# Cross-attention on one core: weights loaded ahead of the context, G made first, Wv and x in pieces of 256 bytes, U in tiles of 32 columns

## The chip, the cores and the metric

One core of a Trainium2 chip, one launch. The time is the device time of an execution in microseconds (us). A kernel's time is the median of its runs. One further execution is profiled; its span, from the first to the last instruction on the core, is a little shorter than its time.

## The reference, cut to what matters

```python
# x: 16 x 256 x 256, ctx_768: 16 x 77 x 192, 8 heads of D = 256, all float32
Q = (x @ Wq).reshape(B, -1, H, D).transpose(0, 2, 1, 3)          # Wq: 256 x 2048
K = (ctx_768 @ Wk).reshape(B, -1, H, D).transpose(0, 2, 1, 3)    # Wk: 192 x 2048
V = (ctx_768 @ Wv).reshape(B, -1, H, D).transpose(0, 2, 1, 3)    # Wv: 192 x 2048
score = jnp.einsum('bhqd,bhkd->bhqk', Q, K) / math.sqrt(D)
score = jnp.where(mask, score, -jnp.inf)
attn = jax.nn.softmax(score, axis=-1)
ctx = jnp.einsum('bhqk,bhkd->bqhd', attn, V).reshape(B, -1, H * D)
out = ctx @ Wo + x                                                # Wo: 2048 x 256
mu = jnp.mean(out, axis=-1, keepdims=True)
var = jnp.var(out, axis=-1, keepdims=True)
return (out - mu) * jax.lax.rsqrt(var + EPS) * gamma + beta
```

## The kernel before, in words

The kernel multiplies the weights with each other first. For each head, G = Wk Wq^T (192 x 256, scaled) and U = Wv Wo (192 x 256). Then the scores are x (G^T c^T), with c the context, and the output is the softmax's weights times (c U). So the work has a **prologue**, which makes G and U once, and a **main loop** over the 16 batches.

The order of every engine's work is the order in which the code issues it (`manual_schedule`, line 83): an engine runs its instructions in order, and each waits on semaphores for what it needs. There are no due times. Transfers are issued by SP, a few by ACT, also in order. Eight completion semaphores are used in turn by the transfers, so an issue waits until the transfer eight before it has landed. PSUM is one pool of eight banks (`ps_mm`, line 92), taken in turn.

The prologue, by lines:

- Loads: the context `c_sb` (449, the first two of 11 row groups by ACT; 450 the rest by SP), then per pair of heads Wq and Wk (458, 459; the first pair in two halves), then Wv in 24 transfers of 64 KB (463), Wo in four of 512 KB (471), the mask, and x of the first four batches (155, eight transfers of 128 KB, by `load_xT`). Wv and x are loaded in blocks of 32 x 32 elements, pieces of 128 bytes, so that VectorE (DVE) can transpose the blocks in place (584, 164).
- `keep_busy` (480 to 484, 487): 22 transposes of the identity into a bank that nobody reads.
- The context's transposes on PE, `pc` (492), with copies to `cA` by ACT, to the upper half of `cB` by DVE, and to its lower half by POOL (498 to 503).
- `turn_qk` (531): per head, four transposes of Wq (`p_wqT`) and four of Wk (`p_wkT`), all at line 524, each with one copy (ACT and DVE in turn, `evacuate`, 135). `pg` (538): two products for rows 0 to 127 of a head's G, issued after the next head's transposes. `ph` (548): the other 64 rows of G, two heads side by side in one bank, tiles of 64 columns.
- `prepare_a` (169) for the first four batches: `pa` (186 from `cA` and `gA`, 200 from `cB` and `gB`). DVE transposes Wv's blocks between the copies (584).
- `pu` and `pw` (538, 548): U by the same helpers, `of_weights` and `rest_of_weights`. Then `pr` (265, 273): the part of c U for the last 13 keys of each batch, which goes by way of DRAM (`scratch`, 287) to `vr` (292).

The helpers for the matrices' shapes: a product "128*32" uses 128 rows and 32 columns of PE's array; four of them beside each other fill the 128 columns. `pa`, `pv`, `ps` and `po` are made in such tiles (BK = 32).

The main loop (632 to 682): per batch the scores `ps` (306) of its two tiles of 128 queries, the softmax on DVE, POOL and ACT, `pv` (228, 239: c U of the batch), `pa` of a batch four ahead, `po` (371), and the normalisation. x of the next four batches is loaded (653) and transposed (671) inside it, and the residual `xg` (131) is loaded four times 1 MB after the prologue's other loads. The tiles `xg` lie on the buffers of the transposed Wq and Wk (510 to 515).

Of the kernel before, what the change touches and what calls it, by code (L numbers as in the profile page):

```python
# [1 line left out]

# [14 lines left out]
P = 128  # L17
# [28 lines left out]
def kernel(  # L46
# [102 lines left out]
    def load_blocks(dst, src):  # L149

        dst = dst.rearrange("p a (m q) -> p a m q", q=BK)
        src = src.rearrange("(m r) (a i q) -> a i r m q", r=BK, q=BK, i=P // BK)
        for a in range(dst.shape[1]):
            for i in range(P // BK):
                nc.sync.dma_start(dst[i * BK : (i + 1) * BK, a], src[a, i])

    def load_xT(g):
        xT_of[g] = in_two("xT", [P, 2, GT * P], g)
        load_blocks(xT_of[g], x.rearrange("b s d -> (b s) d")[g * GT * P : (g + 1) * GT * P, :])

    def transpose_x(g, j):

        cols = xT_of[g][:, :, j * P : (j + 2) * P]
        nc.vector.transpose(cols, cols)
# [4 lines left out]
    def prepare_a(g, pairs, B_first=False):  # L169
# [8 lines left out]
        def cols(dc, i):  # L178
            return slice(dc * P + i * BK, dc * P + (i + 1) * BK)
# [118 lines left out]
    def scores(t):  # L298
# [3 lines left out]
        for m in range(NM):  # L302
            q = j * P + m * BK
            for dc in range(2):
                for i in range(NM):
                    nc.tensor.matmul(  # L306
                        ps[m // 2][i * BK : (i + 1) * BK, m % 2 * 2 * S2 : (m % 2 + 1) * 2 * S2],
                        xT_of[g][:, dc, q : q + BK],
# [134 lines left out]
    with tc.tile_pool(name="wload", bufs=4) as ring, tc.tile_pool(name="wonce", bufs=1) as wp:  # L443
# [3 lines left out]
        wo_r = wo.rearrange("(t p) f -> p t f", p=P)  # L447
        first = 2
        nc.scalar.dma_start(c_sb[:, :first, :], c_rows[:, :first, :])
        nc.sync.dma_start(c_sb[:, first:, :], c_rows[:, first:, :])  # L450
        wq_of, wk_of, wo_of = {}, {}, {}
        wvT = wp.tile([P, H, 2, DL], F32, tag="wvT", name="wvT")
        for n in range(NF):
            wq_of[n] = ring.tile([P, 2, 2 * D], F32, tag="w128", name=f"wq_{n}")
            wk_of[n] = ring.tile([LP, 2, 2 * D], F32, tag="w96", name=f"wk_{n}")
            for lo, hi in ((0, D), (D, 2 * D)) if n == 0 else ((0, 2 * D),):
                cols = slice(2 * n * D + lo, 2 * n * D + hi)
                nc.sync.dma_start(wq_of[n][:, :, lo:hi], wq_r[:, :, cols])
                nc.sync.dma_start(wk_of[n][:, :, lo:hi], wk_r[:, :, cols])
        wv_blocks = wv.rearrange("(m r) (a i q) -> m i r a q", r=BK, q=BK, i=NM)  # L460
        for m in range(DL // BK):
            for i in range(NM):
                nc.sync.dma_start(
                    wvT.rearrange("p h a l -> p (h a) l")[
                        i * BK : (i + 1) * BK, :, m * BK : (m + 1) * BK
                    ],
                    wv_blocks[m, i],
                )
        for n in range(NF):
            wo_of[n] = ring.tile([P, 4, DI], F32, tag="w128", name=f"wo_{n}")  # L470
            nc.sync.dma_start(wo_of[n], wo_r[:, 4 * n : 4 * n + 4, :])
# [12 lines left out]
        keep_busy(20)  # L484
        for r in range(0, NCR, 2):
            if r == first:
                keep_busy(2)
            n = min(2, NCR - r)
            pc = ps_mm.tile([P, 4, P], F32, tag="mm", name=f"pc_{r}")
            for lc in range(2):  # L490
                for j in range(n):
                    nc.tensor.transpose(
                        pc[:, 2 * lc + j, :CR],
                        c_sb[:, r + j, lc * LB : lc * LB + P],
                        ident[:CR, :CR],
                    )
            rows = slice(r * CR, (r + n) * CR)
            evacuate(flat(cA)[:, rows].rearrange("p (j m) -> p j m", m=CR), pc[:, :n, :CR])
            evacuate(
                flat(cB)[LB:, rows].rearrange("p (j m) -> p j m", m=CR),  # L500
                pc[LB:, 2 : 2 + n, :CR],
            )
            nc.gpsimd.tensor_copy(flat(cB)[:LB, rows], flat(cB)[LB:, rows])
        nc.gpsimd.tensor_copy(cRA, cA[:, :, KM:])
        nc.gpsimd.tensor_copy(cRB, cB[:, :, KM:])

# [219 lines left out]
```

## Time and profile before

| | |
|---|---|
| median of 3 runs | 290.67 us (290.23 to 291.16) |
| profiled execution | 290.27 us |
| its span | 288.4 us |
| mean granted PE clock | 0.992 |
| bytes moved | 25.90 MB; 46905 of 64377 packets under 512 bytes |

In the lists, PE is TensorE's products, PEld its weight loads (which run beside products), DVE VectorE, ACT ScalarE, POOL GpSimd, SP the queue that issues transfers. A float32 product appears as two instructions, a transpose as one, so "x32" at line 538 is sixteen products. A line such as `L538 PE MATMUL pu<-wo,wvT 128*128 128x256` reads: line 538, on PE, writes tile pu from tiles wo and wvT, array 128 x 128, moving operand 128 partitions by 256 elements. "[0.80 <-DMA wk]" is idle time of that engine just before, and what ended it. "issue" means that nothing the profile shows was waited for. The chain of work that ended last is followed back from the last instruction, each time to what released it.

### The profile page before, as it was taken

The page shows a single profiled execution, that of the slowest core. Times are in us where ns is not written, and L with a number is a line of the kernel's source. Part 1 is how long each engine was busy: PE and PEld are TensorE (multiplying, and loading weights), DVE is VectorE, ACT ScalarE, POOL GpSimd, SP SyncE. Part 2 cuts the span into 40 slices and gives each one's busy share as a digit, 9 for nine tenths or more (in the row PEclk, how much of TensorE's full clock was granted, in tenths as well). Part 3 has the DMA queues.
Part 4 walks back from the last instruction along what each step waited for, and adds up shares of the span by engine and source line. Part 5 has one row for each costly group of instructions (what it writes and reads, how often), then busy time and mean ns, then how long its engine had stood idle before and what let it go on. Part 6 is the DMA issues. An engine that isn't in the chain of part 4 may idle for free.

```text
span 288.4 us, 11416 instructions
## 1 busy us (share of the span) xinstructions
PE 278.7 (97%) x5132; PEld 177.5 (62%) x5132; DVE 206.3 (72%) x412; ACT 118.2 (41%) x203; POOL 123.7 (43%) x156
## 2 busy tenths in 40 slices
PE   8899999999999999999999999999999999999990
PEld 8795567364656575757575757575757567576550
DVE  0531453435768798989797989897979898898884
ACT  2452232032353535353535353535353534735531
POOL 1800002986554334344334242534342527658562
PEclk9999999999999999999999999999999999999996
DMA  7986798895859401910101009200000000010112
GB/s 201 314 193 95 143 328 117 244 352 147 189 141 139 81 4 39 139 47 5 37 5 35 6 28 142 47 13 25 18 22 22 19 22 24 19 40 2 39 39 73
DMA packets 64377, 25.90 MB, mean 90 GB/s; under 512 B 46905, under 2 KB 62857, under 8 KB 64329
## 3 DMA queue, kind: packets, MB, share of 16 engines
q1 hardware_dynamic: 64088, 25.01, 36.8%
q8 instruction: 40, 0.66, 1.0%
q10 hardware_dynamic: 240, 0.17, 0.2%
q14 instruction: 9, 0.07, 0.1%
HBM read 19.27 MB, written 5.90 MB: 87 GB/s over the span
## 4 chain that ended last, share of the span: by engine, by line
PE 90%; DVE 3%; DMA 3%; SPq 1%; ACT 1%; issue 1%; POOL 0%; POOLq 0%
PE ps L306 23%; PE po L371 22%; PE pa L186 12%; PE pv L228 10%; PE pa L200 6%; PE pv L239 6%; DMA wk<-in_L_xattn_Wk_dram 3%; PE pu L538 2%; PE pr L265 2%; PE pg L538 2%; PE pr L273 1%; PE ph L548 1%; PE pw L548 1%; PE p_wqT L524 1%; PE p_wkT L524 1%; DVE bn L385 1%
## 5 line engine op out<-in xcount | busy, mean ns | idle before, releaser
L328 POOL TENSOR_TENSOR s<-s,top 128x616 f32<-128x616 f32 x32 | 39.0, 1218 | 85.0 <-DVE top L327 77.2
L306 PE MATMUL ps<-a,xT 128*32 128x154 f32 x2048 | 70.0, 294 | 0.0
L306 PEld LDWEIGHTS ps<-a,xT 128*32 128x32 f32 x2048 | 66.4, 110 | 4.0 <-ACT stage L138 0.8
L349 POOL TENSOR_TENSOR p<-e,rden 128x512 f32<-128x512 f32 x64 | 50.4, 808 | 28.6 <-ACT a L664 25.5
L371 PE MATMUL po<-vw,pT 128*32 128x256 f32 x1024 | 61.5, 380 | 0.0
L371 PEld LDWEIGHTS po<-vw,pT 128*32 128x32 f32 x1024 | 31.8, 110 | 28.2 <-issue 5.5
L341 DVE TENSOR_REDUCE den<-e 128x8 f32<-128x616 f32 x32 | 25.5, 795 | 24.2 <-ACT e L335 24.2
L335 ACT ACTIVATE e<-s 128x616 f32<-128x616 f32 x32 | 23.0, 719 | 32.1 <-POOL s L328 32.1
L186 PE MATMUL pa<-cA,gA 128*32 128x308 f32 x512 | 35.8, 423 | 0.0
L320 DVE TENSOR_TENSOR s<-ps,bias 128x308 f32<-128x308 f32 x64 | 27.6, 464 | 7.3 <-POOL bias L617 4.7
L662 ACT COPY vw<-pv 128x512 f32<-128x512 f32 x32 | 18.6, 581 | 32.2 <-PE pv L239 32.2
L228 PE MATMUL pv<-uA,cA 128*32 128x512 f32 x256 | 30.4, 592 | 0.0
L186 PEld LDWEIGHTS pa<-cA,gA 128*32 128x32 f32 x512 | 16.4, 110 | 21.0 <-issue 6.6
L428 DVE SCALAR_TENSOR_TENSOR xg<-xg,rstd,bet 128x256 f32<-128x256 f32 x26 | 28.0, 1078 | 0.9
L396 ACT ACTIVATE std<-mv,eps 128x2 f32<-128x2 f32 (+1 forms) x17 | 5.0, 296 | 57.2 <-DVE mv L388 57.2
L359 DVE STREAM_TRANSPOSE pT<-p 128x640 f32<-128x640 f32 x32 | 25.1, 812 | 2.4 <-POOL p L349 2.4
L327 DVE TENSOR_REDUCE top<-s 128x8 f32<-128x616 f32 x32 | 25.4, 795 | 1.1
L371 PE MATMUL po<-vr,pT 128*32 128x256 f32 x256 | 19.7, 379 | 0.0
L396 ACT ACT_TABLE_LOAD x15 | 19.2, 1283 | 0.3
L200 PE MATMUL pa<-cB,gB 64*32 64x308 f32 x512 | 19.3, 419 | 0.0
L335 ACT ACT_TABLE_LOAD x14 | 18.0, 1283 | 0.2
L599 POOL COPY uB<-uB 64x256 f32<-64x256 f32 x8 | 3.2, 397 | 34.7 <-ACT uB L598 34.3
(75 smaller groups left out, 288.2 us busy)
## 6 DMA issues: line engine op xcount, KB each, us to landing
xT<-in_x_dram SPq DMA_DIRECT2D x32, 128.0 KB
xg<-in_x_dram SPq DMA_DIRECT2D x4, 1024.0 KB
out_dram<-xg SPq DMA_DIRECT2D x15, 256.0 KB
wo<-in_L_xattn_Wo_dram SPq DMA_DIRECT2D x4, 512.0 KB
scratch<-stage SPq DMA_DIRECT2D x16, 104.0 KB
vr<-scratch SPq DMA_DIRECT2D x8, 208.0 KB
wq<-in_L_xattn_Wq_dram SPq DMA_DIRECT2D x3, 512.0 KB
wvT<-in_L_xattn_Wv_dram SPq DMA_DIRECT2D x24, 64.0 KB
```

The costliest lines, as they stand in the source:

```text
L186: nc.tensor.matmul(flat(o[i * BK : (i + 1) * BK]), gA[:, h, cols(dc, i)], flat(cA[:, batches, :]), start=not B_first, stop=B_first,)
L200: nc.tensor.matmul(flat(banks[j + k][i * BK : (i + 1) * BK]), gB[half(k), h // 2, cols(dc, i)], flat(cB[half(k), batches, :]), start=B_fir ...
L228: nc.tensor.matmul(pv[k][i * BK : (i + 1) * BK], cA[:, b, k * BK : (k + 1) * BK], flat(uA[:, heads[i], :]), start=True, stop=False,)
L306: nc.tensor.matmul(ps[m // 2][i * BK : (i + 1) * BK, m % 2 * 2 * S2 : (m % 2 + 1) * 2 * S2], xT_of[g][:, dc, q : q + BK], flat(a_of[g][:, ...
L320: nc.vector.tensor_tensor(s[:, a * H // 2 : (a + 1) * H // 2], ps[a][:, : H // 2 * S2].rearrange("p (h k) -> p h k", k=S2), bias[:, b, :]. ...
L327: nc.vector.tensor_reduce(top, s, AX.X, ALU.max)
L328: nc.gpsimd.tensor_tensor(s, s, top.unsqueeze(2).to_broadcast([P, H, S2]), ALU.subtract)
L335: nc.scalar.activation(e, s_of.pop(t), AF.Exp)
L341: nc.vector.tensor_reduce(den, e, AX.X, ALU.add)
L349: nc.gpsimd.tensor_tensor(part, e_mh[:, :, :, keys], rden_mh.unsqueeze(3).to_broadcast(list(part.shape)), ALU.mult,)
L371: nc.tensor.matmul(po[i * BK : (i + 1) * BK], pT[:, n, i], vw_of[b][:, n // 2, n % 2, :] if n < NF else vr[:, b, :], start=(n == 0), stop= ...
L428: nc.vector.scalar_tensor_tensor(y, y, rstd, bet, ALU.mult, ALU.add)
```

## The change

- **Order.** Wq is loaded by SP and Wk by ACT, ahead of the context, which is now one transfer by SP. PE starts with `turn_qk(0)` and makes G's rows 0 to 127 for all heads and the first half of `ph` before the context's transposes `pc`; the second half of `ph` follows them. `keep_busy` issues ten transposes at the start and none later.
- **Order of d, pieces.** Of a head's 256 values of d, partition block i of 32 holds 64i to 64i + 63, in two parts of 32, in place of 32i to 32i + 31 of each half. So a piece of Wv or x is 64 contiguous elements, 256 bytes. Wv has 24 transfers of the same 64 KB; x has 4 of 256 KB for four batches in place of 8 of 128 KB. `prepare_a` takes G's columns, and Wo's rows are loaded, in this order: Wo comes in 16 transfers of 128 KB (pieces of 1 KB), into one tile `wo_all`, which lies on the buffer of `wq_all` (one tag, one buffer).
- **U in tiles of 32.** `of_weights` has a width: 128 for G, 32 for U. `rest_of_weights` uses 32 for both. U then has 64 products of 128*32 for `pu` in place of 16 of 128*128, and 32 for `pw` in place of 16 of 128*64; `ph` too has 32 in place of 16.

The diff, cut (the helpers that only move are left out):

```diff
     def load_xT(g):
-        xT_of[g] = in_two("xT", [P, 2, GT * P], g)
-        load_blocks(xT_of[g], x.rearrange("b s d -> (b s) d")[g * GT * P : (g + 1) * GT * P, :])
+        xT_of[g] = in_two("xT", [P, GT * NM, 2, BK], g)
+        rows = x.rearrange("b s d -> (b s) d")[g * GT * P : (g + 1) * GT * P, :]
+        rows = rows.rearrange("(m r) (i n) -> i r m n", r=BK, i=NM)
+        for i in range(NM):
+            nc.sync.dma_start(
+                xT_of[g][i * BK : (i + 1) * BK].rearrange("p m n q -> p m (n q)"), rows[i]
+            )
...
         def cols(dc, i):
-            return slice(dc * P + i * BK, dc * P + (i + 1) * BK)
+            return slice((2 * i + dc) * BK, (2 * i + dc + 1) * BK)
...
-                        xT_of[g][:, dc, q : q + BK],
+                        xT_of[g][:, j * NM + m, dc],
...
-        nc.scalar.dma_start(c_sb[:, :first, :], c_rows[:, :first, :])
-        nc.sync.dma_start(c_sb[:, first:, :], c_rows[:, first:, :])
-        wq_of, wk_of, wo_of = {}, {}, {}
-        wvT = wp.tile([P, H, 2, DL], F32, tag="wvT", name="wvT")
+        wk_of = {}
+        wq_all = wp.tile([P, NF, 2, 2 * D], F32, tag="w128", name="wq_all")
+        wq_of = [wq_all[:, n] for n in range(NF)]
+        wvT = wp.tile([P, H, DL // BK, 2, BK], F32, tag="wvT", name="wvT")
         for n in range(NF):
-            wq_of[n] = ring.tile([P, 2, 2 * D], F32, tag="w128", name=f"wq_{n}")
             wk_of[n] = ring.tile([LP, 2, 2 * D], F32, tag="w96", name=f"wk_{n}")
             for lo, hi in ((0, D), (D, 2 * D)) if n == 0 else ((0, 2 * D),):
                 cols = slice(2 * n * D + lo, 2 * n * D + hi)
                 nc.sync.dma_start(wq_of[n][:, :, lo:hi], wq_r[:, :, cols])
-                nc.sync.dma_start(wk_of[n][:, :, lo:hi], wk_r[:, :, cols])
-        wv_blocks = wv.rearrange("(m r) (a i q) -> m i r a q", r=BK, q=BK, i=NM)
+                nc.scalar.dma_start(wk_of[n][:, :, lo:hi], wk_r[:, :, cols])
+        nc.sync.dma_start(c_sb, c_rows)
+        wv_blocks = wv.rearrange("(m r) (h i n) -> m i r h n", r=BK, h=H, i=NM)
         for m in range(DL // BK):
             for i in range(NM):
                 nc.sync.dma_start(
...
+                    wvT[i * BK : (i + 1) * BK, :, m].rearrange("p h n q -> p h (n q)"),
                     wv_blocks[m, i],
                 )
-        for n in range(NF):
-            wo_of[n] = ring.tile([P, 4, DI], F32, tag="w128", name=f"wo_{n}")
-            nc.sync.dma_start(wo_of[n], wo_r[:, 4 * n : 4 * n + 4, :])
+        wo_all = wp.tile([P, H, 2, DI], F32, tag="w128", name="wo_all")
+        wo_rows = wo.rearrange("(h i n c) f -> i n c h f", h=H, i=NM, n=2)
+        for heads in (slice(H // 2), slice(H // 2, H)):
+            for i in range(NM):
+                for n in range(2):
+                    nc.sync.dma_start(
+                        wo_all[i * BK : (i + 1) * BK, heads, n, :], wo_rows[i, n, :, heads]
+                    )
...
-        keep_busy(20)
+        keep_busy(10)
...
+        def of_weights(out, tT, width, moving):
+            for dc in range(2):
+                for lo in range(0, P, width):
+                    nc.tensor.matmul(
+                        out[lo : lo + width],
+                        tT(dc, slice(lo, lo + width)),
+                        moving(dc),
+                        start=(dc == 0),
+                        stop=(dc == 1),
+                    )
...
+            for n in pairs:
+                for dc in range(2):
+                    for i in range(2):
+                        for lo in range(0, LB, BK):
+                            nc.tensor.matmul(
+                                banks[n][i * LB + lo : i * LB + lo + BK],
+                                tT(2 * n + i, dc, slice(P + lo, P + lo + BK)),
+                                moving(2 * n + i, dc),
+                                start=(dc == 0),
+                                stop=(dc == 1),
+                            )
...
+        turn_qk(0)
+        for h in range(H):
+            if h + 1 < H:
+                turn_qk(h + 1)
+            if h % 2 == 0:
+                pg = ps_mm.tile([P, 2, DI], F32, tag="mm", name=f"pg_{h}")
+            of_weights(pg[:, h % 2, :], partial(wk_part, h), P, partial(wq_part, h))
+            if h % 2:
+                nc.scalar.mul(gA[:, h - 1 : h + 1, :], pg, D ** -0.5)
...
+        rest_of_g(range(NF // 2))
         for r in range(0, NCR, 2):
-            if r == first:
-                keep_busy(2)
             n = min(2, NCR - r)
             pc = ps_mm.tile([P, 4, P], F32, tag="mm", name=f"pc_{r}")
...
+        rest_of_g(range(NF // 2, NF))
         for g in range(NG):
             load_x(g)
...
-            of_weights(pu[:, h % 2, :], wvT[:, h], slice(P), lambda dc: wo_part(h, dc))
+            of_weights(pu[:, h % 2, :], partial(wv_part, h), BK, partial(wo_part, h))
```

## The prediction

> **What bounds the kernel now.** I read the busy shares first.
>
> ```profile
> PE 278.7 (97%) x5132; PEld 177.5 (62%) x5132; DVE 206.3 (72%) x412; ACT 118.2 (41%) x203; POOL 123.7 (43%) x156
> ```
>
> TensorE (PE) lacks work for some 10 us of 288.4. The chain of work that ended last says where. Its columns are start, length (us) and what ran.
>
> ```profile
> 3.94 8.76 DMA wk<-in_L_xattn_Wk_dram
> 21.66 1.84 PE pg L538 x8
> 23.50 3.60 PE ph L548 x32
> 27.11 4.28 PE pa L186 x64
> 31.39 4.31 PE pa L200 x128
> 35.70 4.29 PE pa L186 x64
> 39.98 7.10 PE pu L538 x32
> 47.09 3.60 PE pw L548 x32
> 50.69 7.04 PE pr L265 x16
> ...
> 81.69 4.45 PE po L371 x80
> ```
>
> One transfer ends at 12.70, the second piece of Wk (heads 2 and 3). From there to 272 us each piece of the chain on PE begins where the one before ends. So before 12.70 the kernel waits for transfers; after it only PE's own work counts, until the last two batches. A change to any other engine's work past 12.70 gives nothing unless it makes PE wait. What did PE do before 12.70? The timeline (start, length, engine, line, operation) tells.
>
> ```profile
> 5.46 0.82 PEld L492 LDWEIGHTS pc<-ident,c_sb 112*128 112x128 f32 x4
> 6.23 0.42 PEld L482 LDWEIGHTS idle<-ident 128*128 128x128 f32 x2
> 6.70 2.00 PEld L492 LDWEIGHTS pc<-ident,c_sb 112*128 112x128 f32 x18
> 8.65 0.46 PEld L524 LDWEIGHTS p_wqT<-ident,wq 128*128 128x128 f32 x4
> 9.08 0.42 PEld L524 LDWEIGHTS p_wkT<-ident,wk 96*128 96x128 f32 x4
> 12.83 0.52 PE L524 MATMUL p_wkT<-ident,wk 96*128 96x96 f32 x4 [0.80 <-DMA wk<-in_L_xattn_Wk_dram]
> 34.73 1.84 DVE L584 STREAM_TRANSPOSE wvT<-wvT 128x768 f32<-128x768 f32 x2 [0.49 <-DMA wvT<-in_L_xattn_Wv_dram]
> ```
>
> The context's transposes (pc, L492) filled that wait: they cost nothing now, because heads 2 and 3 were not there. The first four take 0.205 us each, the last eighteen 0.111: PE's clock came up at about 6.7 us. The last line says that Wv landed only at 34.73, but the second reading of the chain is that PE did not wait for it. How fast the transfers come is read from the windows view, whose last figure is the mean GB/s from the start to that time.
>
> ```profile
> 0.00:4.05 4.05, 2.70 (x13) 2.71 (x14) 0.06 (x1) 1.28 (x1) 0.80 (x8) 1.00 0.47 131
> 0.00:8.50 8.50, 7.15 (x42) 7.10 (x43) 0.97 (x4) 2.45 (x5) 1.23 (x10) 1.00 0.81 217
> 0.00:9.35 9.35, 8.00 (x50) 7.95 (x51) 1.82 (x6) 3.17 (x7) 2.05 (x12) 1.00 0.84 224
> 0.00:11.40 11.40, 10.05 (x64) 9.57 (x65) 3.30 (x9) 4.34 (x9) 4.03 (x17) 1.00 0.87 243
> ```
>
> Time by rate gives the bytes that had come: 0.53 MB at 4.05, 1.84 at 8.50, 2.09 at 9.35, 2.77 at 11.40. The context is 0.946 MB, two heads of Wq and Wk 0.918 (0.524 + 0.393). Context and four heads, 2.78 MB, had come at 11.44; PE was released at 12.70. So a landing is seen 1.26 us after its last byte.
>
> [...] PE worked from 1.35, and the weight loads halve their time at 6.7, not before. [...] the chain shows no gap over 0.05 us at a change from 128 to 32 columns.
>
> **The change, part by part.**
>
> 1. Order of loading. The two heads that PE waits for no longer have 0.946 MB of context ahead of them. [...] 1.835 MB would do for four heads: they come at 8.47, seen at 9.73. But Wk is on ACT's queue and Wq on SP's. If the engines take from both in turn, Wk runs ahead and Wq has half of what comes until Wk is through, so Wq's 1.049 MB for four heads has come when 2.10 MB have: 9.37, seen at 10.63. That is the later bound. The pieces of Wq and Wk past the first pair have 2 KB, the context's 768 bytes, and the seconds that moved 2 KB pieces show up to 358 GB/s against 267 to 298 for the small ones; so I take 10.3, nearer the later bound. The first pair is no limit: half of it comes at 4.05, seen at 5.3. The third and fourth pair are not waited for: 3.15 MB and 3.67 MB are seen at about 13.9 and 15.6, and PE comes to them 3.3 and 6.6 us after the second, at 13.6 and 16.9 (0.3 us at most, which I leave in the range).
>
> 2. G. From Wk's landing to the end of pg took 12.70 to 23.50, 10.80 us, with one set of four Wq transposes (0.43) already done. From the second pair's landing it is now 11.23. G stays at 128 columns.
>
> 3. The context's transposes come between the halves of ph, with no wait to hide in: 22 x 0.111 = 2.44 us on PE. This is the price of the whole change: its cover is gone. Their copies (ACT 0.35, DVE 0.40, POOL 0.37 a group of four) keep up with PE (0.44), and the second half of ph and the first half of pa lie between the last copy and its reader: nothing for those, 0.8 us if they didn't. ph in tiles of 32: 32 products where 16 of 64 columns were. po gives the price: 40 products of 256 in 4.45 us, 0.111 each, so 3.56 for 3.60. The same.
>
> So pa begins at 10.3 + 11.23 + 1.80 + 2.44 + 1.80 = 27.57, where it began at 27.11: 0.46 us later. The bounds of part 1 give 27.00 and 27.90, -0.11 and +0.79.
>
> 4. keep_busy(10) for 22. Ten at 0.207 end at 3.4, the first weights come at 5.3. PE is idle for 1.9 us in between, so the clock may still be halved in G. Until 10.3 PE can afford that: two heads of transposes (0.79 each at full clock) and one of G (0.87) from 5.3 at half speed, 4.9 us, end at 10.2. After it each microsecond at half speed loses half of one. [...] I take 0.25, with 0 and 1.6 as ends.
>
> 5. U in tiles of 32: 64 products x 0.111 = 7.12 for 7.10, and 32 for pw, 3.56 for 3.60: nothing. Its stationary columns lie together as before.
>
> 6. Wv, x and Wo. Wv in 24 transfers keeps its bytes, in half as many pieces. It moved at 97 GB/s (17.5 to 34 us), x at 112. [...] twice is the other bound. Wq, Wk and the context end at 17.25 as before, since they are the same bytes. So Wv lands by 26.5 to 31.2 where it was 34.7, plus Wo's 2.1 MB at 360 GB/s, 5.8 us: 32 to 37. U begins at 40.4. So this removes 0.49 us of waiting from DVE, which PE never saw: worth nothing. Wo's sixteen transfers wait for the last use of Wq's buffer, at about 19 us, ahead of their turn. x lands some 10 us earlier; its readers start at 61. The loads of xg behind it on SP start earlier too, where only Wo is gone. The x loads in the main loop are hidden before and after. The other order of d changes only which columns are taken, at equal shapes.
>
> 7. ACT's fourth Wk issue waits for the first Wk to land, about 5 us; behind it stand the table load (1.28) and the first copy of Wq, so that copy begins at 6.9. G's first product needs the second head as well, after 8: 1 us of room; if gone, up to 1 us.
>
> Sum: +0.46 + 0.25 = +0.7 us. The profiled execution was 290.27 (span 288.4 and 1.87 around it); it gives 291.0. The median shown is 0.40 above that execution, so 291.4. A measurement of this kernel can tell about 0.3% from no change (0.87 us): this is just inside.
>
> **Rivals.** Slower: the clock stays halved until 13.5, because 22 warming transposes kept PE busy without a break and ten don't. Then 1.6 in place of 0.25: 292.7. It decides from about 11.1 us on (0.4 lost and 0.46 pass 0.87). For it: the 1.9 us gap; against: PE at half speed is full from 5.3 on. Faster: the pairs come in order, at the 358 GB/s of the best second. After the first pair at 5.35 the second needs 2.56 us and is seen at 9.2; with the clock up in time that is 1.1 less than 10.3, 0.65 us under before: 290.0, and past the 0.3% if the landing is seen before 8.95. [...] Late Wv or Wo: sixteen Wo transfers in place of four, issued behind 24 of Wv with eight outstanding; if each piece costs what it does now, Wv lands at 35, Wo at 41: 1 to 2 us lost, 292.9. Last, nothing at all: 290.7, if the landing and the exposed transposes cancel; it is the low end of my own case.
>
> **How the numbers follow.** Forecast 0.54 (290.6 to 292.0), clock 0.25, in-order pairs 0.12, late Wo 0.09. Of the forecast's 0.54, 0.09 lies past 0.87; of the in-order case 0.07 lies past the bound on the fast side. Faster 0.07; same 0.45 + 0.05 = 0.50; slower 0.25 + 0.09 + 0.09 = 0.43. The range reaches from 289.8 (most of the in-order case) to 292.9.
>
> **What would show it.** Right: pc at 0.11 us each behind a half of ph, with no idle PE before it; pa first at 27.3 to 28.3; pu then pw in 10.7 us. Step 1 is wrong if the third head's Wq transposes start before 9.7 or after 10.8; step 4 if PE's weight loads stay at 0.2 us past 11; step 6 if PE waits for Wo or Wv at pu. The prediction fails if PE has idle time past 11 us that isn't there now, or if the main loop's period of 14.5 us changes.

## The result, and the profile after

The changed kernel takes 293.84 us (median of 4 runs, 293.58 to 294.73) where the kernel before takes 290.56 (4 runs, 290.23 to 291.16): the ratio is 1.0116, with a 95% interval from 1.0088 to 1.0143. It is slower by 3.3 us. The forecast was 291.4 with a range to 292.9, so the time lies outside the range. The profiled execution took 293.73 us, its span is 291.9 and the mean granted clock of PE 0.994; before it was 290.27, 288.4 and 0.992. The two profiles differ by 3.46 us, about as the medians do, so they may be compared line by line. (One execution of e1 below was slow, 368.6 us, and counts in no ratio.)

The busy shares come first, as before.

```profile
PE 278.4 (95%) x5280; PEld 175.6 (60%) x5280; DVE 206.3 (71%) x412; ACT 118.2 (40%) x203; POOL 123.7 (42%) x156
```

PE does no more work than before (278.4 us busy for 278.7) in a span that is 3.5 us longer. So the new time is idle time of PE, and the chain of work must show where. Its columns are start, length (us) and what ran.

```profile
1.75 9.17 DMA wk<-in_L_xattn_Wk_dram
...
27.64 4.15 PE pa L184 x64
31.79 4.31 PE pa L198 x128
36.10 4.28 PE pa L184 x64
41.34 4.00 PE pu L515 x64
46.73 3.76 PE pu L515 x64
50.49 3.45 PE pw L530 x64
53.94 7.04 PE pr L263 x16
...
84.94 4.45 PE po L368 x80
```

The reader is to compare each start with the end of the line above. The first `pa` starts at 27.64 (before: 27.11), and up to 40.38 nothing is missing. Then there are two holes that the chain of before doesn't have: `pu` starts at 41.34, 0.96 us after the last `pa` has ended, and its second half at 46.73, 1.39 us after the first half has ended at 45.34. `pr` starts at 53.94 where it started at 50.69, 3.25 us later. The first `po` comes at 84.94 for 81.69, again 3.25: what was lost ahead of `pr` is the whole loss, and the main loop runs as it did.

Who made PE wait? The timeline names the lines around the holes (start, length, engine, line, operation; in brackets the idle time before it and what ended it).

```profile
33.02 9.15 SPq L467 DMA_DIRECT2D wo_all<-in_L_xattn_Wo_dram  x16
...
35.35 1.84 DVE L605 STREAM_TRANSPOSE wvT<-wvT 128x768 f32<-128x768 f32 x2 [0.71 <-DMA wo_all<-in_L_xattn_Wo_dram]
...
41.34 3.99 PE L515 MATMUL pu<-wo_all,wvT 128*32 128x256 f32 x64 [0.96 <-ACT a L139]
...
46.73 3.76 PE L515 MATMUL pu<-wo_all,wvT 128*32 128x256 f32 x64 [1.40 <-DVE uA L141]
```

The first line is SP's queue: it issues the 16 transfers of Wo from 33.02 to 42.17, one each 0.57 us. The second is DVE's transpose of Wv for heads 0 to 3, at 35.35 (before: 34.73), ahead of `pu`; those for heads 4 to 7 run from 40.84 to 42.67, ahead of the second half of `pu`. Wv's last transfer had landed at 35.17. So Wv was there. The releasers in the brackets of the `pu` lines, a copy of `a` and a copy of `uA`, read nothing of Wo. The product waits for several semaphores at once, and the list names the one that came last in the profile; transfers of Wo were under way until after 42.

When each of them landed is on record. The trace has sixteen semaphore marks for each of these transfers, as its shares are done, and it has landed with the last of them. The eight transfers of a half bring in turn the first and the second part of d (n = 0 and n = 1 in the diff) for one quarter of the partitions. The first product of a head reads part n = 0 only, so it needs the 1st, 3rd, 5th and 7th transfer; the next product needs the 8th too. The 7th landed at 41.14, and PE starts at 41.34. The 15th, which is the 7th of the second half, landed at 46.53, and PE starts at 46.73. Both times PE begins 0.20 us after that landing: it waits for Wo. The 8th landed at 41.84, the 16th at 47.17.

The windows view gives the rate. The columns are the stretch, its length, the busy time of PE, its weight loads, DVE, ACT and POOL, PE's clock, the share of the 16 DMA engines that were busy, and GB/s. (The share counts packets that overlap, so it can pass 1.) From 36 to 40 us the core moves little but Wo. Before:

```profile
36.00:40.00 4.00, 4.00 (x65) 1.82 (x57) 2.00 (x4) 1.68 (x4) 0.00 (x0) 1.00 1.07 363
```

After:

```profile
36.00:40.00 4.00, 4.00 (x72) 1.98 (x64) 2.62 (x5) 1.32 (x4) 0.00 (x0) 1.00 0.91 201
```

The same 2.1 MB come at 201 GB/s where they came at 363. At the old rate they take 5.8 us, at the new one 10.4; SP starts to issue them at 33.0, so 43.4 is the earliest end at that rate, and with the landing of the last share it is 47.17.

The sum of the waits: e5 below, where Wo is in time, has `pu` in 6.91 us without a gap. Here it takes 4.00 + 3.76 = 7.76, so 0.85 more is lost inside it. The next product of a half needs the 8th and the 16th transfer, which landed 0.50 us after PE's first start (41.84 for 41.34) and 0.44 after its second (47.17 for 46.73); the lists name no wait there, so that the wait for these two makes up the 0.85 is an estimate from the times. 0.96 + 1.39 + 0.85 = 3.20 us are lost at Wo. Against that stand gains of 0.13 (`pa`, 12.74 for 12.87), 0.19 (`pu`, 6.91 for 7.10) and 0.15 (`pw`, 3.45 for 3.60), and the later start, 0.53: 0.53 + 3.20 - 0.13 - 0.19 - 0.15 = 3.26, where 3.25 are seen.

### The profile page after: what moved, and what is told of

Read it like the earlier page. It is cut to its first block, busy times and chain, and to the rows that moved or that the text cites. A ratio compares the mean times of both kernels' runs of the same rounds, so it can differ in the third digit from the quotient of the medians.

```text
span 291.9 us, 11691 instructions
## 1 busy us (share of the span) xinstructions
PE 278.4 (95%) x5280; PEld 175.6 (60%) x5280; DVE 206.3 (71%) x412; ACT 118.2 (40%) x203; POOL 123.7 (42%) x156
## 4 chain that ended last, share of the span: by engine, by line
PE 90%; DVE 3%; DMA 3%; issue 1%; ACT 1%; POOL 0%; ACTq 0%; POOLq 0%
PE ps L303 23%; PE po L368 21%; PE pa L184 11%; PE pv L226 9%; PE pa L198 6%; PE pv L237 6%; DMA wk<-in_L_xattn_Wk_dram 3%; PE pu L515 3%; PE pr L263 2%; PE pg L515 2%; PE ph L530 1%; PE pr L271 1%; PE pw L530 1%; PE pc L573 1%; PE p_wkT L499 1%
## 5 line engine op out<-in xcount | busy, mean ns | idle before, releaser
L237 PE MATMUL pv<-uB,cB 64*32 64x512 f32 x256 | 17.4, 601 | 0.0
```

Source lines behind the costliest of these rows:

```text
L237: nc.tensor.matmul(pv[k][i * BK : (i + 1) * BK], cB[half(k), b, k * BK : (k + 1) * BK], flat(uB[half(k), heads[i], :]), start=False, stop= ...
```

## The experiments

The theory is that the loss is Wo's loading: its transfers no longer fill 128 partitions, there are 16 in place of 4, and the first product of a half waits until seven of the eight transfers of that half have landed, the next product for the eighth. The rivals are that the new order of loading and of G costs it (with the clock), that the number of transfers alone does it, and that Wv's 24 transfers hold Wo up. All ratios are to the kernel before, run on the same chip, with the 95% interval. Where an expectation has letters, A is the theory of Wo's loading and B a rival, unless it says otherwise.

### Is it the order? (e1)

The kernel before, with only the order part of the change: Wk by ACT, weights ahead of the context, G first, `keep_busy(10)`. Wv keeps its pieces of 128 bytes, Wo its four transfers, U its 128 columns.

```diff
-                nc.sync.dma_start(wk_of[n][:, :, lo:hi], wk_r[:, :, cols])
+                nc.scalar.dma_start(wk_of[n][:, :, lo:hi], wk_r[:, :, cols])
+        nc.sync.dma_start(c_sb, c_rows)
...
+        rest_of_g(range(NF // 2))
         for r in range(0, NCR, 2):
```

> The kernel before with only the order changed: Wq by SP and Wk by ACT ahead of the context, G before the context's transposes, ten warming transposes. Pieces of 128 bytes, Wo in four transfers and U at 128 columns stay as before. Theory A (the loss has two parts: 0.5 us from the order, since pa began at 27.64 instead of 27.11, and 2.7 us from PE waiting for Wo at pu): 0.5 us over before, so 291.1, and no wait of PE at pu. Theory B (the order is the whole loss, because everything behind Wq and Wk in the queue comes later): 3 us over before, so 293.7, with PE waiting at pu.

Measured: 290.79 us against 290.80, ratio 0.9993 (0.9967 to 1.0020). The chain of this kernel:

```profile
27.61 4.28 PE pa L186 x64
31.90 4.31 PE pa L200 x128
36.21 4.28 PE pa L186 x64
40.49 7.10 PE pu L511 x32
...
51.20 7.04 PE pr L265 x16
```

`pa` starts at 27.61, as in the changed kernel, and there is no hole. `pr` is at 51.20, 0.51 us later than before; the time of the whole can't be told from no change. So the order costs about half a microsecond in the chain, as the prediction had it, and the other 2.7 us of the changed kernel come from elsewhere. One profile is good to some 0.3 us here: in e4, which has the code of before up to this point, `pa` starts at 26.84 and not 27.11. But with the new order and the clock up in time it starts at 27.25 to 27.77 in all six profiles (changed, e1, e2, e5, e6, e10).

### Number of transfers or partitions? (e2, e3, e4)

e2 is the changed kernel with Wo in 8 transfers of 256 KB, still on 32 partitions each.

```diff
-        for heads in (slice(H // 2), slice(H // 2, H)):
+        for heads in (slice(H),):
```

> The changed kernel with Wo in 8 transfers of 256 KB on 32 partitions each (all heads in one) in place of 16 of 128 KB. Theory A1 (the number of transfers that SP issues sets Wo's pace, 0.57 us each): the last is issued at about 37.6, Wo is there before PE comes to pu at 40.4, PE waits no more: 2.7 us under the changed kernel, 291.1. Theory A2 (a transfer that writes 32 partitions runs at some 210 GB/s, however many there are): 2.1 MB from 33.5 take 10 us, and the first product now needs all eight, so PE waits once from 40.4 to about 44.8: 4.4 us, and the time is 295.4, above the changed kernel's 293.8.

Measured: 299.09 us, ratio 1.0255 (1.0191 to 1.0319). Half the transfers made it much worse. Timeline, then window:

```profile
46.98 9.97 PE L515 MATMUL pu<-wo_all,wvT 128*32 128x256 f32 x128 [6.47 <-DMA wo_all<-in_L_xattn_Wo_dram]
```

```profile
36.00:40.00 4.00, 4.00 (x68) 1.98 (x64) 2.89 (x5) 1.26 (x3) 0.00 (x0) 1.00 1.13 193
```

SP has issued all eight by 36.9, so no issue is waited for after that. The DMA engines are fully busy (share 1.13) and still move only 193 GB/s (182 to 216 in the stretches of 1 us from 36 to 46). In this order, transfers that fill 32 partitions each come no faster, though the engines are full; in e3 below 32 partitions bring 242. The packets tell the same: those of 1 KB take 93 ns at the median here and 82 in the changed kernel, where on 128 partitions they take 46 (e6, e9, e10). The first product needs the 7th of the eight transfers, which landed at 46.79, so PE waits 6.47 us, and the next needs the 8th, at 48.10. After the wait `pu` takes 9.97 us in place of 6.91. The granted clock is 0.50 from 45.6 to 52.5 us; the part of it with work, 46.98 to 52.45, loses half, about 2.7 us, and some 0.3 are waiting for the 8th. I had expected a wait of 4.4 us and a median of 295.4: the direction was right, the size was not.

e3 and e4 are the kernel before (which keeps its order, its d and its U) with Wo in 16 transfers of 128 KB: in e3 on 32 partitions each, in e4 on 128.

```diff
-            nc.sync.dma_start(wo_of[n], wo_r[:, 4 * n : 4 * n + 4, :])
+            for i in range(NM):
+                part = slice(i * BK, (i + 1) * BK)
+                nc.sync.dma_start(wo_of[n][part], wo_r[part, 4 * n : 4 * n + 4, :])
```

```diff
-            nc.sync.dma_start(wo_of[n], wo_r[:, 4 * n : 4 * n + 4, :])
+            for i in range(4):
+                nc.sync.dma_start(wo_of[n][:, i, :], wo_r[:, 4 * n + i, :])
```

> The kernel before with Wo in 16 transfers of 128 KB, each on 32 partitions and 4 KB per partition, in place of 4 of 512 KB on 128 partitions. Pieces stay at 1 KB. Both theories: the heads are needed one pair after another, so PE hardly waits: 290.6 to 291. What is read is the rate from 34 to 42 us: some 200 to 215 GB/s under A2 (few partitions), 230 under A1 (one issue each 0.57 us); it was 360 before.

> The kernel before with Wo in 16 transfers of 128 KB, each on all 128 partitions with one piece of 1 KB per partition: as many issues and bytes as the run with 32 partitions. A1 (number of transfers): the same rate as with 32 partitions, about 230 GB/s. A2 (partitions): faster, 290 to 360 GB/s. The time is before's, 290.6, under both.

Measured: e3 291.46, ratio 1.0016 (0.9989 to 1.0043), with one wait of 0.34 us ahead of the last quarter of `pu` in its profile; e4 291.31, ratio 1.0008 (0.9985 to 1.0032), with none. The windows, e3 first:

```profile
36.00:40.00 4.00, 4.00 (x92) 1.89 (x77) 2.55 (x4) 0.84 (x2) 0.00 (x0) 1.00 0.86 197
```

```profile
36.00:40.00 4.00, 4.00 (x62) 1.93 (x55) 2.48 (x6) 1.68 (x4) 0.00 (x0) 1.00 0.82 222
```

In this window the partitions make little difference: 197 GB/s on 32 partitions, 222 on 128, both far below 363, and the engines are not full (0.86, 0.82). For e4 I had expected 290 to 360, so that was a miss. The landings and issues show what binds: SP issues these transfers one each 0.475 us at the median, of which the issue itself is 0.43, and 128 KB each 0.475 us are 276 GB/s, so at that pace no more can come. In each window one issue took longer, 1.55 us in e3 and 1.11 in e4. After it e4 has 256 GB/s (40 to 42 us), and e3 this:

```profile
40.00:44.00 4.00, 4.00 (x39) 2.73 (x32) 2.84 (x5) 1.21 (x3) 0.00 (x0) 1.00 0.97 242
```

242 GB/s is more than e2 has in any stretch of 1 us from 36 to 46 (216 at most), from transfers on 32 partitions as well. So 32 partitions are no fixed limit. e3 takes another quarter of the partitions with each transfer, e2 and the changed kernel with every second one; whether that is the reason isn't shown. What e2 shows holds for transfers in its order.

Both things in the theory are thus real, each lowers Wo's rate from 363 to between 180 and 260 GB/s, and neither kernel lost anything that can be measured. (The 0.34 us in e3 say nothing of the cost: its profile is of its slowest execution, 292.93 us, in which `pa` began only at 28.79.) That is a third thing: in the kernel before, two heads need the transfers of one quarter of Wo's heads only, so PE starts with what is there.

### Wo on 128 partitions in the changed kernel (e5, e6)

If d is taken as 2p + n (n = 0, 1; p the partition within a head), a head's rows 2p and 2p + 1 lie on one partition: Wv and x keep their pieces of 256 bytes, and Wo comes on 128 partitions in pieces of 2 KB. e5 is the changed kernel with this, Wo in four transfers; e6 has 16, two per head, in the order in which the heads are used.

```diff
-            return slice((2 * i + dc) * BK, (2 * i + dc + 1) * BK)
+            return slice(2 * i * BK + dc, 2 * (i + 1) * BK, 2)
...
-        wo_rows = wo.rearrange("(h i n c) f -> i n c h f", h=H, i=NM, n=2)
+        wo_rows = wo.rearrange("(h p n) f -> p h n f", h=H, n=2)
+        for k in range(NF):
+            heads = slice(2 * k, 2 * k + 2)
+            nc.sync.dma_start(wo_all[:, heads], wo_rows[:, heads])
```

```diff
+        for h in range(H):
+            for n in range(2):
+                nc.sync.dma_start(wo_all[:, h, n, :], wo_rows[:, h, n])
```

> The changed kernel with the two parts of d interleaved (d = 2p + n in place of 64i + 32n + c), so that Wo can be loaded in 4 transfers of 512 KB on 128 partitions, pieces of 2 KB; Wv and x keep pieces of 256 bytes, U keeps tiles of 32. Stationary operands are then read with a step of 2 elements. Theory A2 (Wo's 32 partitions are what PE waits for at pu): Wo lands by about 41 as in the kernel before, no wait at pu, 2.7 us under the changed kernel: 291.1. Theory C (U in tiles of 32 or the place of Wo on Wq's buffer cost the 2.7 us): no gain, 293.8, with pu's pieces as far apart as in the changed kernel.

> As the run before it, but Wo in 16 transfers of 128 KB on 128 partitions (1 KB pieces): as many issues as the changed kernel. If the number of transfers alone made PE wait at pu, the loss stays: 293.8. If the 32 partitions did (A2), the last of 16 issues 0.55 us apart goes out at 41.8 and each product needs only its own head's two, so no wait: 291.1.

Measured: e5 290.36 us, ratio 0.9993 (0.9976 to 1.0009); e6 290.87, ratio 1.0019 (0.9996 to 1.0043). e5's window and chain:

```profile
36.00:40.00 4.00, 4.00 (x68) 1.97 (x64) 2.25 (x4) 1.55 (x4) 0.00 (x0) 1.00 0.99 363
```

```profile
35.87 4.29 PE pa L184 x64
40.16 6.91 PE pu L512 x128
...
50.52 7.04 PE pr L263 x16
```

Wo comes at 363 GB/s, `pu` follows `pa` at once, and `pr` is 0.17 us earlier than before in spite of the order's half microsecond. All else of the change is in e5: the order, the pieces of 256 bytes, U in tiles of 32, Wo on Wq's buffer, and Wv's pace. Its Wo is issued as late, from 33.07 on, and PE doesn't wait: lateness alone cost nothing. So the loss of the changed kernel is the way in which Wo is loaded, and nothing else. It also prices U: 6.91 + 3.45 = 10.36 for 7.10 + 3.60 = 10.70, a gain of 0.34. e6 moves Wo at 202 GB/s (36 to 40 us), no faster than the changed kernel, and has no wait either (`pu` at 39.99, 6.91 long): with a head that needs two transfers of its own, PE can start while the others come.

### How the loss divides (e9, e10)

Both are e5 with Wo's transfers ordered so that the first product needs more of them. e9 has 8 of 256 KB on 128 partitions, heads 0 and 1 last: the counterpart of e2. e10 has 16 of 128 KB on 128 partitions, in each half the first head last: as many as in the changed kernel, and nearly the same need, seven or eight transfers of a half.

```diff
+        for k in reversed(range(NF)):
+            for n in range(2):
+                heads = slice(2 * k, 2 * k + 2)
+                nc.sync.dma_start(wo_all[:, heads, n, :], wo_rows[:, heads, n])
```

```diff
+        for heads in (range(H // 2), range(H // 2, H)):
+            for h in reversed(heads):
+                for n in range(2):
+                    nc.sync.dma_start(wo_all[:, h, n, :], wo_rows[:, h, n])
```

> The changed kernel with d interleaved (d = 2p + n), Wo in 8 transfers of 256 KB on 128 partitions, pieces of 1 KB, heads 0 and 1 last, so that the first product needs all eight. As many transfers, bytes and pieces as the run with 8 transfers on 32 partitions, and the same need; only the partitions of each differ. If the 32 partitions set the rate there (190 to 210 GB/s): now 330 to 360 GB/s, Wo is there at about 41, PE waits under 1 us: 290.7 to 291.5. If the count or the need of all eight did: a wait of 6.5 us and 297 to 299 as there.

> As above, but Wo in 16 transfers of 128 KB on 128 partitions, each half of the heads in falling order, so that PE needs the first eight for its first product and the other eight for head 4, as in the changed kernel. If the 32 partitions cost the changed kernel its 2.7 us: eight issues 0.55 apart from 33.0 are out at 37.4 and landed by 39, sixteen at 41.8 and landed by 43.4, against 40.2 and 43.8 needed: no wait, 290.7. If count and need did it: waits of about 1 and 1.4 us as in the changed kernel, 293.5.

Measured: e9 293.08, ratio 1.0087 (1.0062 to 1.0111); e10 292.70, ratio 1.0068 (1.0054 to 1.0083). Both are slower than I had expected. e9, window and timeline:

```profile
36.00:40.00 4.00, 4.00 (x92) 1.90 (x79) 2.48 (x4) 0.84 (x2) 0.00 (x0) 1.00 0.94 284
```

```profile
10.13 1.11 PE L497 MATMUL p_wqT<-ident,wq_all 128*128 128x128 f32 x4 [0.85 <-DMA wq_all<-in_L_xattn_Wq_dram]
...
42.62 7.60 PE L513 MATMUL pu<-wo_all,wvT 128*32 128x256 f32 x128 [0.94 <-ACT a L139]
```

With the same number of transfers and the same need, 128 partitions in place of 32 bring 284 GB/s for 193, and `pu` starts at 42.62 for 46.98 in e2. So 32 partitions, taken quarter by quarter, are a cause when transfers are large: the 7th landed at 42.43, in e2 at 46.79. PE waits 0.94 us here and loses 0.69 (7.60 for 6.91) within `pu`; it would have waited longer had it asked in time. It didn't: the third head's Wq transposes take 1.11 us in place of 0.66 (the first line above), so the clock was still halved past 10 us (the granted clock is full from 13.63), and `pa` started at 28.94, 1.3 us after the changed kernel's.

e10, window and timeline:

```profile
36.00:40.00 4.00, 4.00 (x68) 1.98 (x64) 2.09 (x4) 1.26 (x3) 0.00 (x0) 1.00 0.60 176
```

```profile
40.27 3.64 PE L513 MATMUL pu<-wo_all,wvT 128*32 128x256 f32 x64
...
45.38 3.66 PE L513 MATMUL pu<-wo_all,wvT 128*32 128x256 f32 x64 [1.47 <-DMA wo_all<-in_L_xattn_Wo_dram]
```

I had expected no wait at all. The first half is in time; the second waits 1.47 us, about what it waits in the changed kernel (1.39). The sum as above: `pa` starts at 27.71, and 12.74 + 6.91 + 3.45 later, at 50.81, `pr` could start; it starts at 52.50, so 1.69 us are lost at Wo. The same sum for the changed kernel is 27.64 + 23.10 = 50.74 for 53.94, 3.20. So about 1.7 us come from 16 transfers of 128 KB together with the need of most of a half, whatever the partitions, and the other 1.5 from the 32 partitions. The split is read from one profile each, so it is an estimate; the ratios, 1.0068 for e10 and 1.0116 for the changed kernel, divide the loss in a like way. The same sum gives 0.00 for e5 and for e6.

The landings show one thing more. In e10 fifteen of the sixteen shares of the 15th transfer were done at 43.83, in time for the end of the first half of `pu` at 43.91; the last share came at 45.25, and PE started at 45.38. In the changed kernel it is the same: the 7th transfer lacked one share from 39.71 to 41.14, the 15th from 44.90 to 46.53. So one late share in sixteen, by 1.4 to 1.6 us, makes up most of these waits: without it, and all else equal, the changed kernel's first wait would be gone and its second 1.3 us (an estimate from these times: 44.90 + 0.20 less the 43.84 at which PE could have begun). In nine traces (before, changed, e2 to e6, e9, e10) the late share first appears with or just after a packet of 16 KB on a queue named `instruction`, at 35.50 in the changed kernel, and an issue by SP that overlaps that packet takes longer there: 1.34 us in the changed kernel, 1.76 in e10. That this packet is the cause is not shown; no experiment was made on it.

### Does Wv hold Wo up? (e8)

The changed kernel with Wv in 32 transfers of 48 KB, by heads in place of row blocks.

```diff
-        for m in range(DL // BK):
+        for h in range(H):
             for i in range(NM):
                 nc.sync.dma_start(
-                    wvT[i * BK : (i + 1) * BK, :, m].rearrange("p h n q -> p h (n q)"),
-                    wv_blocks[m, i],
+                    wvT[i * BK : (i + 1) * BK, h].rearrange("p m n q -> p m (n q)"),
+                    wv_blocks[h, i],
                 )
```

> The changed kernel with Wv in 32 transfers of 48 KB in place of 24 of 64 KB, pieces of 256 bytes in both. If SP's issue of each transfer sets Wv's pace (0.65 us each, whatever the piece), Wv ends 8 x 0.6 = 5 us later, at about 40, and PE waits for Wo some 5 us more: 298 to 299. If bytes or pieces set it (about 100 GB/s), Wv ends as before at 34.6 and the time is 293.8.

Measured: one execution only, 295.99 us. In its profile the clock was full from 7.4 to 10.8 us and halved again until 14.2, and `pa` came late, so its time isn't compared. Its transfers can be. Windows before, after and here, while Wv comes:

```profile
24.00:33.00 9.00, 9.00 (x150) 4.82 (x154) 1.60 (x4) 1.65 (x5) 0.00 (x0) 1.00 0.56 88
```

```profile
24.00:33.00 9.00, 9.00 (x155) 5.39 (x161) 2.94 (x8) 2.69 (x8) 6.14 (x9) 1.00 0.43 95
```

```profile
24.00:33.00 9.00, 9.00 (x142) 5.61 (x138) 2.97 (x8) 2.81 (x9) 6.03 (x9) 1.00 0.41 92
```

Pieces of 256 bytes lower the share of the DMA engines from 0.56 to 0.43, a factor of 1.3, but Wv comes no sooner: 88, 95 and 92 GB/s. The times of issue show what sets the rate. SP issues these transfers back to back: from one issue to the next the median is 0.67 us before and 0.65 after, for 64 KB, and 0.48 here, for 48 KB; most of it (0.63, 0.61 and 0.44) is the issue itself. These are 98, 101 and 102 GB/s, and one issue of 1.3 to 1.5 us in each window makes them 88 to 95. Only three or four transfers are under way, of the eight that may be, and the engines are less than 60% busy. So Wv's pace is that at which SP issues, and pieces of 256 bytes didn't change it (88 GB/s before, 95 after). Why the issue of one form takes 0.61 us and of another 0.44 isn't shown. With Wo in the changed kernel it is the other way round: there seven or eight are under way from 38.3 to 41.9 us, and each of the last four issues comes 0.01 to 0.02 us after the landing of the transfer eight before. Wo's first issue moved from 33.02 to 35.49 here, so splitting Wv further holds Wo up more.

### Two versions that beat both kernels (e7, e11, e12)

The chain of before waits for Wk's second pair in one piece. Loading it in halves, as the first pair is, should bring the third head sooner. e7 does so for the second pair, e11 for all pairs; both are the kernel before otherwise. e12 adds to e11 what e5 showed to be harmless or good: d as 2p + n with pieces of 256 bytes, Wo in four transfers on 128 partitions, U in tiles of 32. Its order is that of before.

```diff
-            for lo, hi in ((0, D), (D, 2 * D)) if n == 0 else ((0, 2 * D),):
+            for lo, hi in ((0, D), (D, 2 * D)) if n < 2 else ((0, 2 * D),):
```

```diff
-            for lo, hi in ((0, D), (D, 2 * D)) if n == 0 else ((0, 2 * D),):
+            for lo, hi in ((0, D), (D, 2 * D)):
```

> The kernel before with one more pair of heads (heads 2 and 3) of Wq and Wk loaded in two halves, like the first. Nothing else. From the chain of before: PE waits 0.8 to 1.0 us for heads 2 and 3. With halves, head 2 has come when 2.32 MB have (at about 10.1), seen at 11.3, before PE needs it at 11.8. Theory A (only the wait for Wq and Wk and PE's own work bound the prologue): 0.8 to 1.0 us less, 289.8. Rival: four smaller transfers of 1 KB pieces in place of two slow all later ones, so the next pair is late: no gain, 290.7.

> The kernel before with all four pairs of Wq and Wk loaded in halves (a head each), since with only heads 2 and 3 in halves the wait moved to heads 4 and 5. By the bytes: head 4 seen at 14.2, needed at 14.7; head 6 at 17.1, needed at 18.0; head 7 at 18.5, needed at 19.6. Theory A: the wait of 1.0 us is gone for good, pa at 26.1, 289.6. Rival: pieces of 1 KB in place of 2 KB slow the transfers, the wait moves to the last heads: pa at 26.8 again, 290.3.

> The kernel before, its order and its context first, with all pairs in halves, and with the parts of the change that do no harm: d interleaved (d = 2p + n), Wv and x in pieces of 256 bytes, Wo in 4 transfers on 128 partitions with pieces of 2 KB, U in tiles of 32. Theory A: 1.0 us from the halves and 0.35 from U in tiles (pu and pw took 10.36 where they took 10.70): 289.2. Rival: Wv, still paced by its 24 transfers, is late for PE once PE is 1 us earlier: no gain over the run before it.

Measured: e7 291.11 us, ratio 1.0005 (0.9983 to 1.0028); e11 289.74, ratio 0.9951 (0.9926 to 0.9976); e12 289.34, ratio 0.9951 (0.9928 to 0.9974). The chains of e7, e11 and e12:

```profile
8.15 7.53 DMA wk<-in_L_xattn_Wk_dram
...
26.78 4.28 PE pa L186 x64
...
50.36 7.04 PE pr L265 x16
```

```profile
25.75 4.28 PE pa L186 x64
...
38.69 7.14 PE pu L538 x32
...
49.44 7.04 PE pr L265 x16
```

```profile
38.66 6.91 PE pu L535 x128
...
49.02 7.04 PE pr L263 x16
```

In e7 the wait went on to the next pair: a transfer of Wk that ends at 15.68 is now in the chain, and `pa` is only 0.33 us earlier, no more than two profiles of the same code differ (27.11 before, 26.84 in e4). That the next pair would come late is what the rival had. With all pairs in halves no transfer of Wk or Wq is left in the chain, `pa` is 1.36 us earlier and `pr` 1.25 (in its fastest execution, 289.14 us). e12 has `pr` 1.67 earlier. Both are faster than either kernel; between the two the intervals don't decide. Of the changed kernel's parts, U in tiles of 32 is thus worth keeping by the chain, and the order is not; in the time of the whole U's gain can't be told (0.9951 in both).

## Why the prediction was wrong

- **Steps 1 to 3, loading order and G.** Right in their sum: `pa` was to begin 0.46 us later, and begins 0.53 later (e1 alone: 0.50). Of step 1 the picture was not right. It had Wk run ahead of Wq because the two are on two queues; that the DMA engines serve both in turn was a supposition there. In the changed kernel's trace both move at once (0.55 MB of SP's queue and 0.34 of ACT's from 5 to 8 us, 0.43 of each from 8 to 11). The timeline shows the third head's Wq transposes at 9.56 and those of its Wk at 10.96, so Wk was the last, and 0.66 us after the step's 10.3. (9.56 is also before the 9.7 that the prediction had set as a sign that step 1 is wrong.) Which queue is last isn't settled: Wk was in the changed kernel and e2, but in e1, e5, e8, e9 and e10, which load in the same order, Wq ended PE's wait, at 9.98 to 10.72. Two errors cancel: since Wq was already transposed when Wk came, `pg` ends 10.70 us after that landing and not 11.23.
- **Step 4, the clock.** 0.25 us were put down, an estimate of the author's that the trace of before doesn't show. In the profiled execution of the changed kernel none is lost: the clock is full from 8.43, and the transposes of the third head run at full speed. (The prediction's 6.7 us for the kernel before came from a line that joins eighteen weight loads; taken singly they halve at 7.2.) The rival was real, however: in the profiles of e8 and e9, whose prologue up to `pa` is the same, the clock was halved at some time beyond 10 us, and `pa` came at 29.51 and 28.94, 1.9 and 1.3 us later. In e9 it hadn't come up by the first `pg` (1.97 us for 4 instructions, 1.07 at full clock); in e8 it had (1.07) and was halved again after 2.30 us without products; in e10 it had, and stayed up after 1.81 us. So the gap while PE waits for the third head puts the clock at risk: 2.30 us of it cost the clock in e8 (halved from 10.8 to 14.2 us), 1.81 us in e10 did not, and what lies between isn't shown.
- **Step 5, U in tiles of 32.** "Nothing" was 0.34 us of gain. 128 instructions for `pu` took 6.91 us, 0.108 each for 64 products, where 0.111 had been taken from `po`.
- **Step 6, Wo. This is the step that failed.** It said "plus Wo's 2.1 MB at 360 GB/s, 5.8 us: 32 to 37. U begins at 40.4. So this removes 0.49 us of waiting from DVE, which PE never saw: worth nothing." Two terms of this sum are wrong, and one is missing. Wv didn't land at 26.5 to 31.2 but at 35.17, about as before (34.73 is when its reader started there). The 31.2 and the 26.5 were the author's estimates of what pieces of 256 bytes gain, and the trace of before doesn't show them; the engines' share did fall (0.56 to 0.43), but SP's issues set the pace. That alone cost nothing (e5). What cost is the rate. The 360 GB/s were those of four transfers on 128 partitions in pieces of 4 KB; they were carried over to sixteen transfers on 32 partitions, and these ran at 201, while e5's four on 128 partitions ran at 363 and lost nothing. The step moved the bytes and forgot that the new order of d had changed the form of the transfers. So the last transfer landed at 47.17, where PE could have begun the second half at 43.84 (40.38 + 3.46), and 3.20 us were lost at `pu` where the step had put nothing.
- **Missing in step 6: the need.** In the kernel before a head needs one transfer of Wo. After the change each head needs eight, since each transfer brings 32 of the 128 partitions for four heads; the step put this at nothing. e6 and e10 differ in that alone (16 transfers on 128 partitions in both): their ratios are 1.0019 and 1.0068.
- **The rival "late Wv or Wo"** had the place, and Wv at 35, and priced it at 1 to 2 us, 292.9. Its Wo at 41 is still the old rate (5.8 us after 35), and e5 shows that a Wo this late at the old rate costs nothing. So its price came near for another reason: the first half landed at 41.1 to 41.8, but the second at 46.5 to 47.2. It looked at the number of transfers, and not at their partitions.

## What to carry to other kernels

When an edit changes the layout of a tile, look at every transfer that fills the tile: how many partitions one transfer reaches, how many bytes it has, and how many transfers the first reader needs. Look at the landing of a transfer's last share: here PE started 0.20 us after it (41.34 for 41.14, 46.73 for 46.53), and one share of sixteen came 1.4 to 1.6 us after the others. A rate from the profile did not carry over to another form of transfer: 363 GB/s in four on 128 partitions, 201 in sixteen on 32. And where a chain waits for a large transfer at the start, try to cut that transfer, and those behind it too; here it was worth more than the new order: halves for all pairs gave 1.3 us in the chain, halves for one pair no more than two profiles differ by (0.33), and the order cost 0.5.

## What the runs showed of the hardware that was not expected

- Transfers of 256 KB that fill 32 partitions, quarter by quarter, stop at 182 to 216 GB/s with the DMA engines fully busy (share 1.13, e2); the same bytes in as many transfers on 128 partitions reach 284 (e9), in half as many 363 (e5). It is no fixed limit: in e3, with another quarter at each transfer, 242 came on 32 partitions (40 to 44 us).
- SP issues transfers of 128 KB on 128 partitions one each 0.475 us at the median (e4), which is 276 GB/s. With one longer issue among them, 1.1 us in e4 and 1.8 in e10, the windows from 36 to 40 us have 176 to 222 GB/s, with the engines at 0.60 to 0.82 (e10, e4).
- Wv's transfers, pieces of 128 or 256 bytes on 32 partitions, come at about 100 GB/s between pauses, because SP takes 0.65 to 0.67 us from one issue to the next of 64 KB and 0.48 of 48 KB. The share of busy engines fell by 1.3 with the larger pieces (0.56 to 0.43); the rate didn't follow (88 and 95 GB/s).
- One of a transfer's sixteen shares landed 1.4 to 1.6 us after the other fifteen, and the reader waited for it (changed kernel and e10; the cause isn't shown).
- In a wait of 6.47 us (40.51 to 46.98) PE's clock fell: it was granted at 0.50 from 45.6 to 52.5 us (e2), so this wait was paid a second time. Of the 3.06 us that `pu` took longer (9.97 for 6.91), about 2.7 are the halved clock and some 0.3 the wait for the last transfer.
- A gap of 2.30 us without products, to 10.72 us, cost the clock, which was halved from 10.8 to 14.2 (e8: the four transposes after the gap took 1.09 us); one of 1.81 us, to 10.20, did not (e10: they took 0.66).
